# Images 3 and 4 in the 4x4 convolution, later query blocks with the probabilities stationary, and steps placed by an account of emitted work

## The chip, the cores and the metric

The kernel runs on one core of a Trainium2 chip. The metric is the device time of one execution in microseconds (us); the time of a kernel is the median of its runs. The engines are named as the profile names them: PE (TensorE, the matmuls), PEld (its weight loads), DVE (VectorE), ACT (ScalarE), POOL (GpSimd) and SP (SyncE, which here only issues DMAs). Every tensor is float32; PE does one float32 matmul as two passes, and the profile counts passes.

## The reference

Four images of 256 channels and 64x64 pixels go through four layers, each `x = x + layer(groupnorm(x))`:

- layer 0: a 3x3 convolution 256 to 256, group norm, relu (`xs`); then attention over all 4096 pixels with 128 channels, `y = softmax(theta^T phi) g`; a 1x1 convolution back to 256 channels, group norm, times 0.1, plus `xs`.
- layer 1: linear attention with 4 heads of 32 channels; q is normalised over its channels and k over the pixels, `context = k v^T`, `out = context q`, a 1x1 convolution, an RMS norm.
- layer 2: a depthwise 3x3 convolution and a 1x1 convolution whose weights are generated from pooled features of the image.
- layer 3: a 1x1 convolution whose weights are a mixture of 4 experts, with the mixture from a small softmax over the image's mean.

## The kernel before

**Tiles and stages.** Images are numbered b = 0 to 3 in the code. An image is held as 2 halves of 128 channels on the partitions. `convolve_first` does the first image's convolution alone. Then, for b = 0, 1, 2, `attend(b)` (layer 0's attention) runs together with a side chain: `tail(b-1)` (layers 0's end, 1, 2 and 3 of the image before) and the convolution of image b+1. `attend(3)` runs with `tail(2)`; `tail(3)` comes last and alone. Between the stages `project` computes theta, phi and g of the next image.

**Attention.** `attend` has 8 query blocks (q) of 512 pixels and in each 16 steps (m). A step computes the logits of the next step (`pf`, 2 matmuls of 512 columns; ACT takes the exponent into `pr`), then 2 matmuls of 512 columns with 128 columns of g as the stationary operand and `pr` moving, summed into `py` (L1129), and DVE adds `pr` (128x1024) to a running sum `tot`. At a block's end `ended_by_dram` turns the sums of all partitions through DRAM into reciprocals, multiplies `py`, and projects it with `ww` (`ps_wy`); the last block of an image uses `ended` (L1081) instead: a matmul with ones (`pss`), and a reciprocal of 128x512 on DVE. `ended_by_dram` is a generator: one of its steps is taken in each attention step.

**Convolution.** A fast convolution over tiles: `down` combines rows (DVE), `across` combines columns (DVE) into `v`, PE multiplies `v` with transformed filters `u` (`ps_conv`), `joined` and `joining` combine the products back (DVE). The second image's (`convolve_second`) has tiles of 4x4 outputs: 6 rows a x 3 pairs of columns, 8 matmuls of 256 columns for a pair (L601). The third and fourth (`convolve`) have 4x2 outputs: 6 x 4 products of 4 matmuls of 512 columns (L529). In `convolve_second` the output lies in `xp` by phases, and its relu pieces (L698) are 4 ACT instructions of 256 columns; for the other images a piece is one instruction of 1024 (L703). Two of the 8 pieces are issued at the end of the convolution, one after each of the first six steps of `project`.

**The order of the work.** It is written out by hand: each engine executes its instructions in the order in which the Python code issues them. `run(chain, attention)` takes one attention step for each step of the side chain. The side chain is a generator; it yields how many attention steps are to pass, and `Chain.steps` (L82) adds these up, times a rate, and passes whole steps:

```python
credit += n * self.rate
while credit >= 1:
    credit -= 1
    yield
    self.tick()
```

The rates are 1.33 for b = 0, 0.83 for b = 1 and 2, and 1.2 for b = 3. `yield None` passes exactly one step. `w.later(n, f)` issues f after n further steps. `linear_attention` goes through 8 chunks of 512 pixels twice: `qk_of`, `turned`, `context` in the first loop (yields of 1.0 a chunk), `outputs`, `added`, `scaled` in the second (0.6 + 0.6 a chunk). `mixed` computes the softmax of the experts (`ps_log`), mixes the weights on DVE (`wm`, two halves; yields of 2.9 in all), and multiplies (`ps_ex`). For b = 2 `mixed` issues only a small bias matmul (`bias`, `ps_b`) and puts the 16 products into `held`; `tail(3)` takes them out by `fill` where it has gaps.

**Buffers.** There are 8 PSUM banks under one name (`bank`), 9 tiles of 128x1024 (`k4`) and 4 of 128x512 (`k2`).

Of the kernel before, what the change touches and what calls it, by code (L numbers as in the profile page):

```python
# [13 lines left out]
P = 128  # L14
NH = 2
# [23 lines left out]
RW = MX * (IX + 1)  # L39

# [5 lines left out]

class Chain:
# [3 lines left out]
    def __init__(self, layers, rate=1.0, held=()):  # L51
        self.layers, self.rate, self.due = layers(self), rate, []
        self.held, self.unsettled = held, []
# [28 lines left out]
    def steps(self):  # L82
        credit = 0.0
        for part in (self.layers, self.pending()):
            for n in part:
                if n is None:
                    credit += self.rate - 1
                    yield
                    self.tick()
                    continue  # L90
                credit += n * self.rate
                while credit >= 1:
                    credit -= 1
                    yield
                    self.tick()


@with_exitstack
def conv_preact_fast(ctx: ExitStack, tc: tile.TileContext, guard, x, wc, wtpg, ww, wqkv, wout, w1cat, wd2,
# [3 lines left out]
    nc = tc.nc  # L103
    B = x.shape[0]
# [26 lines left out]
    def tt(o, a, b, op):  # L131
        nc.vector.tensor_tensor(o, a, b, op)  # L132

    def stt(o, a, s, b, op0, op1):
        nc.vector.scalar_tensor_tensor(o, a, s, b, op0, op1)  # L135
# [8 lines left out]
    tpg = cp.tile([P, 3, N], F32, name="tpg")  # L144
    ra = cp.tile([P, NH, IY, RW], F32, name="ra")
    rt = cp.tile([P, NH, IY, RW], F32, name="rt")
    theta, phi, g = tpg[:, 0, :], tpg[:, 1, :], tpg[:, 2, :]
# [57 lines left out]
    def block_average(name, k):  # L205

        member = sp.tile([P, P // k], F32, name=name + "_m", bufs=1)
        nc.vector.tensor_reduce(member, ident.rearrange("p (g k) -> p g k", k=k), AX.X, ALU.add)
        t = cp.tile([P, P], F32, name=name)
        nc.vector.tensor_scalar(t.rearrange("p (g k) -> p g k", k=k),  # L210
# [18 lines left out]
    def scale_weights(w):  # L229


        nc.vector.tensor_scalar(bo_s, bo_s, 1.0 / HEADS, None, ALU.mult)

        nc.vector.tensor_scalar(gains, vec_s[:, V_GN:V_GN + 2, :], float(NH * P) ** 0.5, None, ALU.mult)
        for h in range(NH):
            nc.vector.tensor_scalar(wqkv_s[:, h, :], wqkv_s[:, h, :], gains[:, 0, h:h + 1], None, ALU.mult)
# [3 lines left out]
        for h in range(NH):  # L240
            sq = k2("wsq")
            nc.scalar.activation(sq[:, 0:2 * HID], wqkv_s[:, h, 0:2 * HID], AF.Square)
            yield 1
            nc.tensor.matmul(ps[:, 0:2 * HID], ones, sq[:, 0:2 * HID], start=(h == 0), stop=(h == NH - 1))
        wmax = sp.tile([P, 1], F32, name="wmax", bufs=1)
        nc.vector.tensor_reduce(wmax, ps[:, 0:2 * HID], AX.X, ALU.max)
        for side in range(2):
            nc.vector.tensor_scalar(guard[:, side, B * NQ:B * NQ + 1], wmax, GUARD_MAX[side] / NORM2_MAX, None, ALU.mult)

# [4 lines left out]
    tpgf = tpg.rearrange("p k n -> p (k n)")  # L254
# [7 lines left out]
    def filter_down(rows):  # L262

        for h in range(NH):
            w = [taps[:, h, i, :] for i in range(3)]
            if rows == (0,):
                nc.scalar.mul(u1[:, 0, h], w[0], 1 / 4)
            elif rows == (5,):
                nc.scalar.copy(u1[:, 5, h], w[2])
            elif rows == (1, 2):  # L270
                ends, mid = k4("ends")[:, 0:3 * NH * P], k4("mid")[:, 0:3 * NH * P]
                nc.scalar.mul(mid, w[1], 1 / 6)
# [3 lines left out]
            else:  # L276
                far, mid = k4("far")[:, 0:3 * NH * P], k4("mid2")[:, 0:3 * NH * P]
                nc.scalar.mul(far, w[2], 1 / 6)
                nc.scalar.mul(mid, w[1], 1 / 12)
# [8 lines left out]
    def filter_across(a):  # L288
# [9 lines left out]
        nc.scalar.mul(mid, ends[:, :, 1], 0.5)  # L298
# [36 lines left out]
    def stats_tile():  # L335
        return sp.tile([P, NH, 8, 6], F32, name="st")

    def aggregated(st):
        mv = sp.tile([P, NH, 2], F32, name="mv")
        for h in range(NH):  # L340
            nc.vector.bn_aggr(mv[:, h, :], st[:, h, :, :].rearrange("p c s -> p (c s)"))
        return mv

    def warm(n):

        if n:
            ps = bank("ps_warm")
            for i in range(2 * n):
                nc.tensor.matmul(ps[:, 0:P], ones, ident, start=(i == 0), stop=(i == 2 * n - 1))

    def group_finish(st, avg, eps, shift=None, between=(), idle=(0, 0)):
# [12 lines left out]
        nc.tensor.matmul(pm[:, 0:NH], avg, mv[:, :, 0], start=True, stop=True)  # L364
# [5 lines left out]
        nc.vector.tensor_copy(gm, pm[:, 0:NH])  # L370
# [9 lines left out]
        nc.tensor.matmul(pv[:, 0:NH], avg, ev, start=True, stop=True)  # L380
        rstd = sp.tile([P, NH], F32, name="rstd")
        nc.vector.tensor_scalar(rstd, pv[:, 0:NH], eps, None, ALU.add)  # L382
# [12 lines left out]
    def affine(gm, rstd, gw, gb, before, factor):  # L395
# [7 lines left out]
        if factor != 1.0:  # L403
            nc.vector.tensor_scalar(sc, sc, factor, None, ALU.mult)
            nc.vector.tensor_scalar(sh, sh, factor, None, ALU.mult)
# [86 lines left out]
    def load_filter(a, k, last):  # L492

        u = filter_tile("u")
        (nc.scalar if last == 3 else nc.sync).dma_start(out=u, in_=rows_d[a, :, :, 0 if k == 0 else 2] if k in (0, last) else filters[a, :, k - 1])
        return u
# [13 lines left out]
    def joiner(st, factor=None):  # L510
# [4 lines left out]
        def stats(k):  # L515
            for oh in range(NH):
                for s in range(2):
                    nc.vector.bn_stats(st[:, oh, 2 * k + s, :], image[:, oh, bass.ts(s, IY // 2), k, :])
# [5 lines left out]
        def products(a, k, v, u):  # L524

            ps = [bank("ps_conv") for _ in range(NH)]
            for oh in range(NH):
                for h in range(NH):
                    nc.tensor.matmul(ps[oh], u(oh, h), v[:, bass.ts(h, 512)], start=(h == 0), stop=(h == NH - 1))  # L529
                if k == 1:  # L530
                    one[oh] = k2("one").rearrange("p (y x) -> p y x", x=IX1)
                    p = ps[oh].rearrange("p (y x) -> p y x", x=IX1)
                    if factor is None:
                        nc.scalar.copy(one[oh], p)
                    else:
                        nc.scalar.mul(one[oh], p, factor)
# [21 lines left out]
        def row_products(a, rows):  # L558

            banks = []  # L560
            for oh in range(NH):
                if a != 5:
                    take(a, oh)
                for s in range(2):
                    ps = bank("ps_row").rearrange("p (y x) -> p y x", x=HW)
                    for n in range(NH * 3):
                        h, j = divmod(n, 3)
                        nc.tensor.matmul(ps, u1[:, a, h, j * NH * P + oh * P:j * NH * P + (oh + 1) * P],
# [3 lines left out]
                    else:  # L572
                        nc.scalar.copy(dst[oh][:, bass.ts(s, RB), :], ps)
# [11 lines left out]
    def planar_joiner(st):  # L585

        parts = {}

        def stats(k):
            for oh in range(NH):  # L590
                for s in range(2):
                    nc.vector.bn_stats(st[:, oh, 2 * k + s, :], outs[:, oh, k, bass.ts(s, 2), :])

        def products(pair, v, u):

            banks = []
            for i in range(2):
                ps = bank("ps_conv")
                for oh in range(NH):
                    for h in range(NH):  # L600
                        nc.tensor.matmul(ps[:, bass.ts(oh, IY * IX)], u[i][:, h, bass.ts(oh, P)],  # L601
# [1894 lines left out]
```

## Time and profile before

| what | us |
|---|---|
| median of 3 runs (lowest, highest) | 3007.39 (3007.21, 3008.11) |
| the profiled execution | 3005.05 |
| its span, first to last instruction | 3003.3 |
| PE busy / DVE busy / ACT busy in the span | 2953.0 / 2058.4 / 1192.8 |
| attention of image 0 with its side chain | 181.1 to 696.6: 515.5 |
| attention of image 1 with its side chain | 743.6 to 1422.5: 678.9 |
| attention of image 2 with its side chain | 1466.7 to 2145.6: 678.9 |
| attention of image 3 with `tail(2)` | 2189.8 to 2754.0: 564.2 |
| `tail(3)` alone, to the end | 2754.0 to 3003.3: 249.3 |

A line of the profile gives the code line, the engine, the operation, output <- inputs by name and shapes, the number of instructions, the time an engine was busy with them and the mean duration in ns, then the time that the engine sat idle just before them and what it waited for. Matmuls are pipelined: a matmul's duration is longer than the distance to the next, so costs are taken from the distance of starts. In a timeline a row begins with its start and its duration in us and merges equal instructions that follow each other.

### The profile page before, as it was taken

The page shows a single profiled execution, that of the slowest core. Times are in us where ns is not written, and L with a number is a line of the kernel's source. Part 1 is how long each engine was busy: PE and PEld are TensorE (multiplying, and loading weights), DVE is VectorE, ACT ScalarE, POOL GpSimd, SP SyncE. Part 2 cuts the span into 40 slices and gives each one's busy share as a digit, 9 for nine tenths or more (in the row PEclk, how much of TensorE's full clock was granted, in tenths as well). Part 3 has the DMA queues.
Part 4 walks back from the last instruction along what each step waited for, and adds up shares of the span by engine and source line. Part 5 has one row for each costly group of instructions (what it writes and reads, how often), then busy time and mean ns, then how long its engine had stood idle before and what let it go on. Part 6 is the DMA issues. An engine that isn't in the chain of part 4 may idle for free.

```text
span 3003.3 us, 25088 instructions
## 1 busy us (share of the span) xinstructions
PE 2953.0 (98%) x8750; PEld 1511.7 (50%) x8750; DVE 2058.4 (69%) x2835; ACT 1192.8 (40%) x2318; POOL 132.3 (4%) x182
## 2 busy tenths in 40 slices
PE   7999999999999999999999999999999999999998
PEld 3454555555565444444566444444546644444744
DVE  8747667773646994778455797578655468886585
ACT  2234333335456333322455533412335454333732
POOL 0000000001001000000001000000000100000100
PEclk9999999999999999999999999999999999999999
DMA  5245534224402225431610334243431222244021
GB/s 225 76 98 114 60 60 77 39 35 100 90 4 36 32 25 140 86 72 35 161 8 11 53 20 88 78 88 67 89 101 14 25 42 46 28 95 91 22 70 68
DMA packets 536133, 200.58 MB, mean 67 GB/s; under 512 B 471040, under 2 KB 481024, under 8 KB 532480
## 3 DMA queue, kind: packets, MB, share of 16 engines
q1 hardware_dynamic: 127808, 163.25, 17.6%
q10 hardware_dynamic: 403584, 18.88, 12.0%
q0 software_dynamic: 4608, 16.78, 3.7%
q8 instruction: 71, 1.16, 0.2%
q14 instruction: 62, 0.51, 0.1%
HBM read 130.13 MB, written 85.52 MB: 72 GB/s over the span
## 4 chain that ended last, share of the span: by engine, by line
PE 81%; DVE 12%; issue 5%; ACT 1%; POOL 0%; DMA 0%; DVEq 0%; POOLq 0%; ACTq 0%
PE pf L1021 25%; PE py L1129 24%; PE ps_conv L529 5%; PE ps_tp L957 4%; PE ps_qk L1303 3%; PE ps_ex L1804 3%; PE ps_pw L1577 3%; DVE tot L132 2%; DVE dw L135 2%; PE ps_conv L601 2%; PE ps_ctx L1330 2%; PE ps_g L962 2%; PE ps_o L1399 2%; PE ps_wy L1073 2%; PE ps_dw L1624 1%
## 5 line engine op out<-in xcount | busy, mean ns | idle before, releaser
L1022 ACT ACTIVATE pr<-pf 128x512 f32<-128x512 f32 x1024 | 603.1, 596 | 1092.0 <-PE pf L1021 1034.3
L1021 PE MATMUL pf<-tpg 128*128 128x512 f32 x2048 | 966.3, 594 | 0.0
L1129 PE MATMUL py<-pr,tpg 128*128 128x512 f32 x2048 | 961.7, 592 | 0.0
L132 DVE TENSOR_TENSOR tot<-tot,pr 128x1024 f32<-128x1024 f32 x448 | 546.5, 1220 | 181.8 <-ACT pr L1022 181.0
L1129 PEld LDWEIGHTS py<-pr,tpg 128*128 128x128 f32 x2048 | 389.2, 190 | 489.7 <-issue 481.6
L1021 PEld LDWEIGHTS pf<-tpg 128*128 128x128 f32 x2048 | 383.0, 190 | 428.4 <-issue 407.3
L135 DVE SCALAR_TENSOR_TENSOR dw<-xp,dk,dw 128x1008 f32<-128x1008 f32 x208 | 263.1, 1268 | 6.7 <-ACT dw L1569 3.6
L529 PE MATMUL ps_conv<-v,u 128*128 128x512 f32 x384 | 170.9, 593 | 3.2 <-DVE v L132 3.2
L132 DVE TENSOR_TENSOR tpg<-ps_g,bg_s 128x512 f32<-128x512 f32 x32 | 22.1, 692 | 146.9 <-PE ps_g L962 146.9
L529 PEld LDWEIGHTS ps_conv<-v,u 128*128 128x128 f32 x384 | 72.8, 190 | 95.8 <-issue 89.1
L957 PE MATMUL ps_tp<-big,wtpg_s 128*128 128x512 f32 x256 | 116.3, 594 | 2.7 <-ACT big L698 2.0
L225 POOL TENSOR_TENSOR rstd<-rstd,half 128x2 f32<-128x2 f32 x24 | 17.5, 729 | 2194.4 <-DVE rstd L382 2070.5
L1303 PE MATMUL ps_qk<-wqkv_s,xg 128*128 128x256 f32 x496 | 113.1, 379 | 0.0
L1303 PEld LDWEIGHTS ps_qk<-wqkv_s,xg 128*128 128x128 f32 x496 | 94.0, 190 | 21.3 <-issue 8.6
L1577 PE MATMUL ps_pw<-dw,pk 128*128 128x512 f32 x216 | 98.0, 593 | 0.9 <-DVE dw L135 0.9
L958 ACT ACTIVATE tpg<-ps_tp,btp_s 128x512 f32<-128x512 f32 x64 | 44.0, 687 | 95.3 <-PE ps_tp L957 95.3
L957 PEld LDWEIGHTS ps_tp<-big,wtpg_s 128*128 128x128 f32 x256 | 46.6, 190 | 54.5 <-issue 45.2
L1313 ACT ACTIVATE qk<-ps_qk,rinv 128x256 f32<-128x256 f32 x100 | 46.9, 474 | 65.2 <-PE ps_qk L1303 62.9
L962 PEld LDWEIGHTS ps_g<-wtpg_s,big 128*128 128x128 f32 x512 | 62.2, 192 | 15.3 <-issue 15.3
L132 DVE TENSOR_TENSOR v<-ra 128x1024 f32<-128x1024 f32 x58 | 69.2, 1221 | 0.3
L1812 ACT ACTIVATE res<-ps_ex,b 128x512 f32<-128x512 f32 x56 | 38.2, 687 | 76.0 <-PE ps_ex L1804 72.4
L1577 PEld LDWEIGHTS ps_pw<-dw,pk 128*128 128x128 f32 x216 | 40.9, 190 | 53.2 <-issue 49.7
(391 smaller groups left out, 3099.0 us busy)
## 6 DMA issues: line engine op xcount, KB each, us to landing
xp<-in_x_dram SPq DMA_DIRECT2D x16, 1024.0 KB, 8.1
xs_d<-big POOLq DMA_DIRECT2D x32, 512.0 KB, 6.4
wy_d<-wt SPq DMA_DIRECT2D x32, 512.0 KB, 2.8
wy<-wy_d SPq DMA_DIRECT2D x32, 512.0 KB, 4.0
out_dram<-res SPq DMA_DIRECT2D x64, 256.0 KB, 2.0
xs_d<-in_x_dram SPq DMA_DIRECT2D x24, 512.0 KB, 6.0
xs<-xs_d SPq DMA_DIRECT2D x24, 512.0 KB, 4.7
wp<-in_wp_dram SPq DMA_DIRECT2D x16, 512.0 KB, 5.3
```

The lines of the kernel that those rows point to most:

```text
L132: nc.vector.tensor_tensor(o, a, b, op)
L135: nc.vector.scalar_tensor_tensor(o, a, s, b, op0, op1)
L529: nc.tensor.matmul(ps[oh], u(oh, h), v[:, bass.ts(h, 512)], start=(h == 0), stop=(h == NH - 1))
L601: nc.tensor.matmul(ps[:, bass.ts(oh, IY * IX)], u[i][:, h, bass.ts(oh, P)], v[:, i, bass.ts(h, IY * IX)], start=(h == 0), stop=(h == NH - 1))
L957: nc.tensor.matmul(ps, wtpg_s[:, h, k, :], big[:, h, cols], start=(h == 0), stop=(h == NH - 1))
L962: nc.tensor.matmul(ps[:, j, :], big[:, h, bass.ts(4 * c + j, P)], wtpg_s[:, h, 2, :], start=(h == 0), stop=(h == NH - 1))
L1021: nc.tensor.matmul(pf, phi[:, bass.ts(2 * m + s, P)], theta[:, bass.ts(q, 512)], start=True, stop=True)
L1022: nc.scalar.activation(pr[:, bass.ts(s, 512)], pf, AF.Exp)
L1129: nc.tensor.matmul(py, g[:, bass.ts(2 * m + s, P)], probs[i][:, bass.ts(s, 512)], start=(m == 0 and s == 0), stop=(m == NM - 1 and s == 1))
L1303: nc.tensor.matmul(ps[:, 0:2 * HID], xg[:, h, bass.ts(j, P)], wqkv_s[:, h, 0:2 * HID], start=(h == 0), stop=(h == NH - 1))
L1577: nc.tensor.matmul(ps, pk[:, h * NH * P + oh * P:h * NH * P + (oh + 1) * P], dw[h][:, bass.ts(s, 512)], start=(h == 0), stop=(h == NH - 1))
L1804: nc.tensor.matmul(ps, wm[h][:, bass.ts(oh, P)], big[:, h, bass.ts(c, 512)], start=(h == 0), stop=(h == NH - 1))
```

## The change

1. Images 2 and 3 (the third and fourth) go through the 4x4 convolution too: `convolve(w, b, pace)` is the former `convolve_second`, and all three later images have the relu in 4 instructions a piece. Its filters are loaded from SP's queue; the copies of x into `xs_d` move into the first loop of `linear_attention` for images 2 and 3. One more step is passed between two pairs whose products aren't issued (`begun`).
2. In `attend` a block is done "across" if it is the last of its image, or from block 3 on in images 1 and 2 (12 of the 32 blocks): a 128x128 part of the probabilities is the stationary operand, and 129 columns of g move, of which the last is ones. `tot` falls away. `ended` takes the sums from the 129th column, scales, and turns the result with 4 transposes.
3. Statistics move from DVE to ACT: the sums come from `accum_out`, the squares from `Square` on ACT, in `nonlocal_out`, in `pointwise_added` and for three quarters of the convolution's output.
4. Side steps in attention are placed by an account instead of the yielded numbers. Every instruction issued through `on_pe`, `on_dve`, `on_act` adds an estimate of its time. A float yielded by the side chain no longer passes steps; an integer or None passes that many; beyond that, attention steps pass only while DVE or ACT is more than 2 us behind PE in the account. `behind` never falls below -4.

The core of the diff:

```diff
+TURNED = 3
+class Load:
+    SPARE, AHEAD = 2.0, 4.0
+    def add(self, kind, us):
+        if kind == PE:
+            self.products += us
+            for k in (DVE, ACT):
+                self.behind[k] = max(self.behind[k] - us, -self.AHEAD)
+        else:
+            self.behind[kind] += us / self.share[kind]
+    def full(self):
+        return max(self.behind[DVE], self.behind[ACT]) > self.SPARE
+class Metered:
+    def us(self, name, args, kw):
+        if self.kind == PE:
+            n = max(columns(args[2] if name == "matmul" else args[0]), P)
+            return n / (600.0 if name == "matmul" else 1200.0) / (HT if args[0].shape[0] == HP and n > P else 1)
+        n = columns(args[1] if name in ("tensor_reduce", "bn_stats", "bn_aggr") else args[0])
+        if self.kind == DVE:
+            return 0.12 + n * (0.0065 if name == "reciprocal" else 0.0011) + (0.08 if "accum_out" in kw else 0)
+        return 0.12 + n * 0.00102 + (0.19 if "accum_out" in kw else 0)
...
     def steps(self):
+        if self.load is not None:
+            self.load.share, self.load.behind = self.share, [0.0] * 3
         for part in (self.layers, self.pending()):
             for n in part:
...
+                for _ in range(1 if n is None else n if isinstance(n, int) else 0):
                     yield
                     self.tick()
+                while self.load.full():
+                    done = self.load.products
                     yield
                     self.tick()
+                    if self.load.products == done:
+                        break
...
         def piece(c, h):
-            if b == 1:
+            if b > 0:
...
+            if begun:
+                yield 1
+            w.later(1, lambda a=a, pair=pair, v=v, u=u, after=lambda us=us, i=i: load_filter_of(us, i + 1, 1): multiply(a, pair, v, u, after))
+            begun.append(i)
+            yield slow
...
-        def ended(q, py, tot, xc):
+        def ended(q, py, xc):
+            total, r = (sp.tile([P, 4], F32, name=name) for name in ("total", "r_q"))
+            for i in range(2):
+                on_dve.tensor_copy(total[:, bass.ts(i, 2)], py[i][:, :, P])
+            on_dve.reciprocal(r, total)
+            yn = k2("yn")
+            tt(yn[:, 0:2 * P].rearrange("p (t o) -> p t o", o=P), py[0][:, :, 0:P],
+               r[:, 0:2].unsqueeze(2).to_broadcast([P, 2, P]), ALU.mult)
+            for t in range(2, 4):
+                on_act.activation(yn[:, bass.ts(t, P)], py[1][:, t - 2, 0:P], AF.Copy, scale=r[:, t:t + 1])
...
             yield
+            pt, yt = bank("ps_yt"), k2("yt")
+            for t in range(4):
+                on_pe.transpose(pt[:, bass.ts(t, P)], yn[:, bass.ts(t, P)], ident)
...
+        def across(q):
+            return q == NQ - 1 or 0 < b < B - 1 and q >= TURNED
...
+                if across(q):
+                    for t in range(4):
+                        on_pe.matmul(py[t // 2][:, t % 2, :], probs[i][:, s * 512 + t * P:s * 512 + (t + 1) * P], g[:, 2 * m + s, :],
+                                  start=(begin and t % 2 == 0), stop=(end and t % 2 == 1))
+                else:
+                    on_pe.matmul(py, g[:, 2 * m + s, 0:P], probs[i][:, bass.ts(s, 512)], start=begin, stop=end)
...
+    FIRST, MIDDLE, LAST = (1.0, 0.75, 0.9), (1.0, 0.86, 0.91), (1.0, 0.75, 0.85)
-            run(Chain(both(*parts), 1.33 if b == 0 else 0.83).steps(), attention)
+            run(Chain(both(*parts), load, FIRST if b == 0 else MIDDLE).steps(), attention)
-        run(Chain(tail(B - 2, big, qT, held=held), 1.2).steps(), attention)
+        run(Chain(tail(B - 2, big, qT, held=held), load, LAST).steps(), attention)
```

`ended_by_dram` also passes one more step between its multiply on DVE (`yq`) and the projection. The account isn't used in `convolve_first` and in `tail(3)`.

## The prediction

> **What bounds the kernel.** I read the page's busy times and its chain first:
>
> ```profile
> PE 2953.0 (98%) x8750; PEld 1511.7 (50%) x8750; DVE 2058.4 (69%) x2835; ACT 1192.8 (40%) x2318; POOL 132.3 (4%) x182
> ...
> PE 81%; DVE 12%; issue 5%; ACT 1%; POOL 0%; DMA 0%; DVEq 0%; POOLq 0%; ACTq 0%
> ```
>
> Busy PE need not be PE at its peak, so I took from the timeline of PE how far apart matmuls start (start, duration, line, count):
>
> ```profile
> 1124.62 3.60 PE L1577 MATMUL ps_pw<-dw,pk 128*128 128x512 f32 x8
> 1128.05 1.88 PE L1021 MATMUL pf<-tpg 128*128 128x512 f32 x4
> ...
> 1444.13 1.95 PE L962 MATMUL ps_g<-wtpg_s,big 128*128 128x128 f32 x16
> 1445.92 3.60 PE L957 MATMUL ps_tp<-big,wtpg_s 128*128 128x512 f32 x8
> ...
> 2340.59 1.91 PE L1330 MATMUL ps_ctx<-xt,qk 128*128 128x257 f32 x8
> 2342.34 1.89 PE L1303 MATMUL ps_qk<-wqkv_s,xg 128*128 128x256 f32 x8
> 2344.06 1.88 PE L1021 MATMUL pf<-tpg 128*128 128x512 f32 x4
> ```
>
> A pass of 512 columns costs 3.43/8 = 0.429 us, of 256 columns 1.72/8 = 0.215 (0.216 over all), of 257 columns 0.219, of 128 columns with a new weight load each 1.79/16 = 0.112; a transpose pass 0.109. Summing these prices over the recorded passes gives 2920 of 3003 us, and in the four attention stages the starts follow each other at these distances but for some 5 us a stage. The waits of PE say the same (us in total, times, longest):
>
> ```profile
> PE ps_conv L529 <- DVE v L132: 3.2, 2, 1.6
> PE pv L380 <- DVE ev L132: 2.5, 6, 0.8
> PE ps_wy L1073 <- DVE yq L132: 2.2, 2, 1.1
> PE ps_tp L957 <- ACT big L698: 2.0, 3, 0.7
> ```
>
> So the time is PE's work plus PE's few waits. Less DVE work gains nothing by itself; what counts is how many passes go or come, and whether PE still finds its operands ready.
>
> [...] the trace has 190 ns a load, yet 112 ns from load to load. [...]
>
> **Part 1, the convolution.** By-form groups of PE:
>
> ```profile
> L529 PE MATMUL ps_conv<-v,u 128*128 128x512 f32 x384 | 170.9, 593 | 3.2 <-DVE v L132 3.2
> L601 PE MATMUL ps_conv<-v,u 128*128 128x256 f32 x288 | 65.1, 379 | 0.0
> ```
>
> An image goes from 192 passes x 0.429 = 82.4 to 288 x 0.216 = 62.2 us; two images: **-40.4**. DVE's combining grows from 68 instructions of 1024 columns at 1.22 and 48 of 512 at 0.69 (116 us) to 50 and 120 (144 us) an image; attention's own PE work hides it, and uncovered it would be 28 us an image. The relu in four pieces: in the second image's `project` PE waits at `ps_tp` for ACT's `big` L698 in three places, 2.5 us beyond the distance of starts; the images with one instruction a piece have none. Two more images: **+5.0**. Filter loads take 3.1 us to landing and products lie at least 7 apart (a step of 3.43 and their own 3.46): nothing. The copies into `xs_d` (6 us each on SP's queue) move into a stretch in which SP has nothing that PE waits for: nothing; late, they would hold the first reload of a block's sums.
>
> **Part 2, across.** One step of a half: 2 passes x 0.429 = 0.858 become 4 x 2 passes of 129 columns. No row shows 129. From `ps_g` (0.112) and the step from 256 to 257 columns I take 0.113: 0.904, +0.045. [...] 12 blocks x 32 = 384: **+17.3** (+8 to +33). Transposes 12 x 4 x 0.109 = +5.2, the four `pss` pairs gone -3.4: **+1.8**. DVE loses 12 x 15 adds of 1.22 = 220 us, worth nothing on PE. At the very end `fill(2)` (3.43 us) now stands between the transposes and `ps_wy`; before, it stood behind `ps_wy` and covered the reciprocal of 3.36. Last statistics about **+2** (0 to 3).
>
> **Part 3, statistics.** Twice in a tail, 16 `Square`s with their accumulator reads (0.72 + 0.19, as L1595 in the last image) replace 16 `bn_stats` of 0.69. That is 29 us more of ACT a tail beside 675 us of PE, of which ACT is busy for 266 now; it would count only before the sums are read, where a forced step of 3.43 stands. Nothing.
>
> **Part 4, the account.** I added up the side chains with the diff's own formulas. For b = 0 DVE has 352 us, /0.75 = 469, under 492 of PE; for b = 1 and 2 it is 429/0.86 = 499 under 632 (the rest are forced steps); for b = 3 354/0.75 = 472 under 524. All end before attention does (after 118 to 122 of 128 steps), so nothing runs over; an overrun would cost its DVE time. But where PE's side work pays for ACT's and DVE's in the account, no step passes at all, and `behind` forgets that DVE can't start until PE's newest product is there. Three places:
>
> (a) `mixed`. The two forced steps before leave `behind` at -4. After `ps_log` DVE gets 4.36 us of account, /0.86 = 5.1: `behind` reaches 1.1, under 2, no step; with 0.75 it reaches 1.8, no step either. Before, 2.9 x 0.83 = 2.4 steps stood there. What the wait is without steps, the last image shows, where held products fill it:
>
> ```profile
> 2961.53 0.38 PE L1765 MATMUL ps_log<-rw_s,hb 64*128 64x4 f32 x2
> ...
> 2965.21 0.29 DVE L132 TENSOR_TENSOR wm<-wm,ident 128x128 f32<-128x128 f32 x1
> 2965.42 0.35 DVE L1785 TENSOR_SCALAR wm<-ex,scales 128x256 f32<-128x256 f32 x1
> ...
> 2967.36 0.29 DVE L132 TENSOR_TENSOR wm<-wm,ident 128x128 f32<-128x128 f32 x1
> ```
>
> First half ready after 4.0 us, second after 6.1. For the tails of images 0 and 1 PE waits 4.0 - 0.2 = 3.8 (the first half's products then cover the second); for image 2 `bias` needs both: 5.9. PE's queue behind it, attention included, waits. **+13.5**.
>
> (b) Second loop of `linear_attention`. Before, one step (3.43) stood in each chunk:
>
> ```profile
> 896.14 1.04 PE L1429 MATMUL ps_zt<-ident,z 128*128 128x128 f32 x8
> ...
> 897.02 1.89 PE L1399 MATMUL ps_o<-w,xp 128*128 128x256 f32 x8
> 898.75 1.88 PE L1021 MATMUL pf<-tpg 128*128 128x512 f32 x4
> 900.46 1.88 PE L1129 MATMUL py<-pr,tpg 128*128 128x512 f32 x4
> 902.18 1.04 PE L1429 MATMUL ps_zt<-ident,z 128*128 128x128 f32 x8
> ```
>
> PE's own work is 2.6 a chunk. ACT's loop is longer: four squares 2.04, DVE and POOL 1.25, `scaled` 0.8, together 4.1. A chunk gives the account 3.5 us of DVE, /0.86 = 4.1, against 2.6 of PE, so the credit of 4 carries the first three chunks (two for b = 2) and one late one without a step. The first `z` is ready 5.2 after its `ps_o` starts, when PE has had 3.5 of work: 1.7; then 4.1 - 2.6 = 1.5 each; half of that late. 1.7 + 1.5 + 1.5 + 0.8 = 5.5 for b = 1 and again for b = 2; for the chain of b = 3, 3.2: **+14.2** (0 to 25).
>
> (c) First loop: 6.5 us of PE a chunk (16 passes of 0.216, 12 transposes of 0.109, 8 passes of 0.219) against a loop of 6.1 from transposes through squares, POOL, DVE's two `xt` and its normalising, 7.0 where POOL's `pow` takes 1.9; PE's 6.5 exceed ACT's 5.1/0.91 in the account, so no step passes at all. 1 us a tail: **+3** (0 to 10).
>
> Gone, by the distance of starts: 1.27 us at `ps_wy` (extra step) and 1.78 at the first `ps_conv`, in two stages each, **-6**.
>
> **Sum.** -40.4 + 5.0 + 17.3 + 1.8 + 2 = -14.3 of work and fixed waits; 13.5 + 14.2 + 3 - 6 = +24.7 of waits. Span 3003.3 + 10.4 = 3013.7. The median shown stands 4.1 above the profiled span (3007.39 - 3003.3): **3018 us**, own range 3008 to 3030.
>
> **Rivals.** My new waits sum to 30.7 us. Up to 14.3 the kernel ends faster by 6 or more, above 26.3 slower by 6; my forecast stands only 4.4 beyond. *PE stays fed*: the places of part 4 cost nothing, because PE comes to them with its queue full and DVE and ACT ahead, and only the old waits go. For it: alone, in the last image, the first loop ran its later chunks without a wait. Against it: PE is in order and can't overtake a product that waits. 3007.4 - 14.3 - 6.0 = 2987, and with some 4 us of small waits, as a stage has now, **2991**: faster. *Weight loads show*: with sixteen loads in a row for whole blocks, 129 columns cost 0.118: 384 x 8 x 0.005 = +15, 3033; at 0.125, 3055. `ps_g` speaks against it, but only in bursts of 16. *Waits for banks*: two `py` leave six PSUM banks for all else across, and four at a block's change; a wait of 0.2 us in every second of the 192 steps is +19, 3037. Against it: `py` and `ps_ctx` leave six already, without waits. *The account does nothing*: can't be; 2.4 steps in `mixed` become none by arithmetic.
>
> **Chances.** A measurement can tell about 0.2% (6 us) from no change. Forecast 0.52 (of it 0.07 within 6 us of before, 0.02 faster), PE stays fed 0.27 (0.21 faster, 0.05 same, 0.01 slower), weight loads 0.12, buffers 0.09 (0.04 of these two the same, 0.01 faster). Faster 0.24, same 0.16, slower 0.60. Range: 2988 takes in the fed case, 3038 the lesser half of the other two: 2988 to 3038.
>
> **What would show it.** Right: 576 `ps_conv` passes of 256 columns 0.216 apart and none at 512 in images 2 and 3; `py` across 0.113 apart; waits of `ps_zt` for `z`, and of `ps_ex` and `ps_b` for `wm`, of 4 to 6 us each in the list of PE's waits; `ps_tp` waits for `big` 9 times; no `pf` among the chunks of the first loop. Wrong: attention steps inside `mixed`, an attention stage of image 1 much below 680 us (I have 678.9 - 20.2 + 7.2 + 1.3 + 7.2 = 674.4), or PE's busy starts 0.12 apart in across blocks.

## The result and the profile after

The kernel after takes 3049.61 us (median of 4 runs, 3047.57 to 3053.32), the kernel before beside it 3007.75 (3007.21 to 3008.27): a ratio of 1.0142, 95% interval 1.013 to 1.0155. It is slower by 42 us. The profiled execution took 3053.32 us, the longest of the four; its span is 3051.5: 48.2 more than before.

The page of the kernel after, busy times and two groups of PE (out<-in, shapes, count, then busy time and mean ns, then PE's idle time ahead of them). Every metered operation now has the line of the helper that records it, L99, so the groups go by names:

```profile
PE 2950.8 (97%) x11286; PEld 1762.6 (58%) x11286; DVE 1833.7 (60%) x2808; ACT 1335.4 (44%) x2674; POOL 121.1 (4%) x185
...
L99 PE MATMUL py<-tpg,pr 128*128 128x129 f32 x3072 | 377.6, 277 | 10.4 <-ACT pr L99 10.4
...
L99 PE MATMUL ps_conv<-v,u 128*128 128x256 f32 x864 | 197.8, 382 | 5.8 <-DMA u<-rows_d 3.2
```

DVE lost 225 us of work, as the change has it, and PE's busy time hardly moved. But priced by pass, as in the prediction (0.4295 for 512 columns, 0.216 for 256 or 257, 0.112 for 128 or 129, 0.109 for a transpose), PE's work fell from 2919.9 to 2895.4 us, by 24.5. What lies beyond these prices between the starts rose from 60.2 to 132.3, by 72.1. All of the loss, and more, is waiting or slow passes. The list of PE's waits (us in total, times, longest) says where:

```profile
PE pm L99 <- DVE mv L99: 23.3, 6, 16.9
PE ps_zt L99 <- DVE z L99: 15.5, 9, 2.8
PE py L99 <- ACT pr L99: 11.9, 6, 5.2
PE ps_ex L99 <- DVE wm L99: 7.3, 2, 3.6
PE ps_b L99 <- DVE wmh L99: 5.1, 2, 3.6
PE ps_tp L99 <- ACT big L99: 4.7, 7, 0.7
PE ps_zt L99 <- ACT junk L99: 4.5, 2, 2.3
PE ps_xt L99 <- DVE xg L99: 3.4, 3, 1.2
PE ps_conv L99 <- DMA u<-rows_d: 3.2, 2, 2.3
```

The first row stood there before too, with 22.2 us. The waits for `z`, `wm`, `wmh` and `xg` are among those forecast. Those of `py` for `pr` and of `ps_conv` for a filter were not.

The wait in `mixed`, tail of image 0, in the timeline of PE, and the same stretch by windows (length, busy time and count by engine, granted clock of PE ahead of the DMA share):

```profile
1138.11 0.38 PE L99 MATMUL ps_log<-rw_s,hb 64*128 64x4 f32 x2
1142.13 5.30 PE L99 MATMUL ps_ex<-big,wm 128*128 128x512 f32 x8 [3.64 <-DVE wm L99]
```

```profile
core 0: us, PE busy (x) PEld busy (x) DVE busy (x) ACT busy (x) POOL busy (x), PEclk, DMA share, GB/s
1138.60:1142.00 3.40, 0.00 (x0) 0.00 (x0) 2.77 (x11) 0.35 (x2) 0.00 (x0) 1.00 0.00 0
1142.00:1145.40 3.40, 3.27 (x4) 1.52 (x5) 2.09 (x6) 0.00 (x0) 0.00 (x0) 0.50 0.00 0
```

`ps_ex` starts 4.02 after `ps_log`, of which 0.16 is the pass itself: 3.86 of wait, three times in the run. And then something that the prediction has nowhere: in the 3.4 us after the wait PE's granted clock is 0.50 and only 4 passes of 512 columns fit in, where 8 would at 0.4295 each. Before, the recorded clock has no such window between the first microseconds and the last; now it has 13, in 11 stretches, in mid-run, and by the passes in them they cost 18.4 us.

The second new wait, in the timeline of ACT and PE, where image 2's convolution begins:

```profile
1188.01 8.69 ACT L99 ACTIVATE big<-xp,nb,rstd 128x1024 f32<-128x1024 f32 x4 [2.56 <-DVE nb L99]
```

```profile
1188.38 1.95 PE L99 MATMUL py<-tpg,pr 128*128 128x129 f32 x16
1190.16 1.88 PE L99 MATMUL pf<-tpg 128*128 128x512 f32 x4
1197.23 3.81 PE L99 MATMUL py<-tpg,pr 128*128 128x129 f32 x16 [5.19 <-ACT pr L99]
1200.83 3.17 PE L99 MATMUL pf<-tpg 128*128 128x512 f32 x4
```

Four pieces of `normalise_planar` stand in ACT's queue ahead of attention's exponent, 8.69 us: it starts at 1196.59, behind the last piece, though the `pf` it reads ran from 1186.58 for 1.96 us. `py` waits 5.35. Again the passes after it go at half clock: 16 passes of 129 columns take 3.60 from start to start (1200.83 - 1197.23), and 1.78 before the wait (1190.16 - 1188.38), 0.111 a pass.

### The profile page after: what moved, and what is told of

Same layout as the page of the kernel before. It is cut to its first block, busy times and chain, and to the rows that moved or that the text cites. A ratio compares the mean times of both kernels' runs of the same rounds, so it can differ in the third digit from the quotient of the medians.

```text
span 3051.5 us, 30579 instructions
## 1 busy us (share of the span) xinstructions
PE 2950.8 (97%) x11286; PEld 1762.6 (58%) x11286; DVE 1833.7 (60%) x2808; ACT 1335.4 (44%) x2674; POOL 121.1 (4%) x185
## 4 chain that ended last, share of the span: by engine, by line
PE 85%; issue 6%; DVE 4%; ACT 3%; DMA 2%; POOL 1%; SPq 0%; POOLq 0%; DVEq 0%; ACTq 0%
PE py L99 28%; PE pf L99 27%; PE ps_conv L99 6%; PE ps_ex L99 4%; PE ps_tp L99 4%; PE ps_pw L99 3%; PE ps_qk L99 3%; PE ps_wy L99 2%; PE ps_ctx L99 2%; PE ps_g L99 2%; PE ps_dw L99 1%; ACT big L99 1%; ACT junk L99 1%; PE ps_o L99 1%; DVE st L99 1%
## 5 line engine op out<-in xcount | busy, mean ns | idle before, releaser
L99 ACT ACTIVATE pr<-pf 128x512 f32<-128x512 f32 x1024 | 601.0, 596 | 976.9 <-PE pf L99 951.4
L99 PE MATMUL pf<-tpg 128*128 128x512 f32 x2048 | 973.8, 599 | 0.0
L99 PE MATMUL py<-pr,tpg 128*128 128x512 f32 x1280 | 602.3, 593 | 1.5 <-ACT pr L99 1.5
L99 PEld LDWEIGHTS pf<-tpg 128*128 128x128 f32 x2048 | 378.8, 192 | 380.4 <-issue 367.1
L99 DVE TENSOR_TENSOR tot<-tot,pr 128x1024 f32<-128x1024 f32 x280 | 342.1, 1222 | 170.8 <-ACT pr L99 170.3
L99 PEld LDWEIGHTS py<-tpg,pr 128*128 128x128 f32 x3072 | 376.4, 194 | 101.7 <-issue 84.4
L99 PEld LDWEIGHTS py<-pr,tpg 128*128 128x128 f32 x1280 | 243.9, 191 | 309.5 <-issue 298.1
L99 PE MATMUL py<-tpg,pr 128*128 128x129 f32 x3072 | 377.6, 277 | 10.4 <-ACT pr L99 10.4
L99 DVE SCALAR_TENSOR_TENSOR dw<-xp,dk,dw 128x1008 f32<-128x1008 f32 x208 | 263.1, 1269 | 7.0 <-ACT dw L99 3.6
L99 PE MATMUL ps_conv<-v,u 128*128 128x256 f32 x864 | 197.8, 382 | 5.8 <-DMA u<-rows_d 3.2
L99 PEld LDWEIGHTS ps_conv<-v,u 128*128 128x128 f32 x864 | 162.3, 191 | 36.8 <-issue 11.6
L99 PE MATMUL ps_tp<-big,wtpg_s 128*128 128x512 f32 x256 | 117.1, 596 | 4.7 <-ACT big L99 4.7
L99 DVE TENSOR_TENSOR tpg<-ps_g,bg_s 128x512 f32<-128x512 f32 x32 | 22.1, 692 | 155.2 <-PE ps_g L99 155.2
L99 PE MATMUL ps_qk<-wqkv_s,xg 128*128 128x256 f32 x496 | 112.1, 379 | 0.0
L99 PEld LDWEIGHTS ps_qk<-wqkv_s,xg 128*128 128x128 f32 x496 | 94.0, 190 | 13.8 <-issue 1.4
L99 PE MATMUL ps_pw<-dw,pk 128*128 128x512 f32 x224 | 101.0, 593 | 0.0
L99 DVE SCALAR_TENSOR_TENSOR sums<-ps_conv,sums 128x512 f32<-128x512 f32 x72 | 49.8, 691 | 77.1 <-PE ps_conv L99 65.5
L99 DVE BATCH_NORM_STATS2 wy_st<-wt 128x6 f32<-128x512 f32 x64 | 43.8, 692 | 74.4 <-ACT wt L99 73.9
L99 PEld LDWEIGHTS ps_tp<-big,wtpg_s 128*128 128x128 f32 x256 | 45.9, 191 | 54.6 <-issue 42.3
L99 ACT ACTIVATE tpg<-ps_tp,btp_s 128x512 f32<-128x512 f32 x64 | 44.0, 687 | 70.5 <-PE ps_tp L99 70.5
L99 ACT ACTIVATE res<-ps_ex,b 128x512 f32<-128x512 f32 x56 | 38.1, 688 | 79.1 <-PE ps_ex L99 77.2
```

The lines of the kernel that those rows point to most:

```text
L99: return f(*args, **kw)
```

## The experiments

Differences below are to the changed kernel's median, 3049.7 (3049.61, and 3049.77 when it ran again), each with the ratio to the kernel before on the same chip.

**Theory.** The account lets no step pass where PE's side work pays for DVE's and ACT's, PE runs into the wait of `mixed`, of the second loop of `linear_attention` and of `normalise_planar`, and each of these waits costs a second time through half clock. **Rivals.** Steps are a fixed stock (128 an image), so that a wait mended at one place comes up at another; the waits come from the new work itself (the planar convolution, the across blocks), whatever places it; half clock is a side effect without a price.

**Steps in `mixed`.**

```diff
                 if j % 2 == 1:
-                    yield 0.6
+                    yield 1 if w.load is not None and h == 0 else 0.6
```

> The changed kernel, but two attention steps are forced inside `mixed` between the first half's scaled experts and its first product (tails of images 0, 1, 2). Theory, zero steps: the three waits behind ps_log (3.86 us each, and 1.66 more for the second half in the tail of image 2) go, and with them the three stretches of half TensorE clock after them (1.6, 1.4 and 2.5 us lost): 3 x 3.86 + 1.66 + 5.4 = 18.6 us less, 3031. If only the waits count and the half clock is no cost of theirs: 3036. Rival, the waits only move, because the steps spent here are missing later: 3045 to 3052.

Measured: 3029.64 us, ratio 1.0074 (1.0057 to 1.0091), 20 us less where 18.6 were expected. In PE's timeline the same place now holds attention:

```profile
1137.60 0.38 PE L99 MATMUL ps_log<-rw_s,hb 64*128 64x4 f32 x2
1137.92 1.98 PE L99 MATMUL pf<-tpg 128*128 128x512 f32 x4
...
1145.03 1.45 PE L99 MATMUL ps_ex<-big,wm 128*128 128x512 f32 x3
```

Two steps are forced, and the chain ends one step later, after 123 of 128: the account passes one step fewer further on. So the steps were there to be had, and the rival of a fixed stock falls at this place. The two timelines also show that what stands behind a waiting product waits with it: issued ahead of `ps_ex`, `pf` starts 0.32 us after `ps_log`; issued behind it, no pass at all runs for 3.86 us.

**Steps in the second loop of `linear_attention`.**

```diff
             zb = outputs(c)
             root(zb[0])
-            yield 0.6
+            yield 1 if c in range(NC) else 0.6
```

> The changed kernel, but one attention step is forced in each of the eight chunks of the second loop of linear_attention (tails of images 0, 1, 2). Theory, zero steps: the waits of ps_zt for z (7.5, 8.6 and 4.6 us) go, and the four stretches of half clock after them (1.3, 1.7, 1.6, 1.5 us lost): 20.7 + 6.1 = 27 us less, 3023. Waits alone: 3029. Rival, the steps are missing later or the loop is held by something else than its lack of steps: above 3040.

Measured: 3025.69 us, ratio 1.0064 (1.0047 to 1.0081), 24 us less where 27 were expected. No wait of `ps_zt` for `z` over 0.5 us is left in the tails of images 0 to 2. The waits of `mixed` stand where they were (7.3 us of `ps_ex` for `wm`), and `py`'s longest is 5.7 for 5.2.

**Steps between the pieces of `normalise_planar`.**

```diff
                     on_act.activation(to, src, AF.Identity, bias=nb[:, h:h + 1], scale=rstd[:, h:h + 1])
-            yield 0.6
+            yield 1 if q in (0, 1, 2) else 0.6
```

> The changed kernel, but an attention step is forced after each of the first three of the four pieces of normalise_planar. Theory: the 5.35 us for which py waits for pr in images 1 and 2 come from ACT, which has four copies of 2.17 us queued ahead of attention's Exp; with a step between the pieces both waits go, and the half clock after them (2.95 and 1.40 us lost): 10.7 + 4.4 = 15 us less, 3035. Rival, py waits for another reason (banks, DVE): 3047 to 3052.

Measured: 3034.12 us, ratio 1.0093 (1.0077 to 1.011), 15.6 us less where 15 were expected. `py` waits for `pr` no longer at this place. The account prices such a piece on ACT at 0.12 + 1024 x 0.00102 = 1.16 us; it took 8.69/4 = 2.17.

**Copies moved.** The copies of image 1 into `xs_d` go out of the convolution's loop:

```diff
-            if b == 1 and i % 3 == 2 and i < 12:
-                copy_x(b, i // 3)
...
             if a + 2 < TY:
                 loaded.append(load(a + 2))
+            if a < 4:
+                copy_x(1, a)
```

> The changed kernel, but the eight copies of image 1 into xs_d leave the convolution's loop and are issued in filters_across, four times two, earlier in the same attention stage. Theory: the four waits of ps_conv in the stage of image 0 (0.75, 1.04, 2.48, 2.16 us, each some 5 us after a copy) come from a filter load queued behind 2 x 512 KB on SP; they go, with 1.5 us of half clock after the last: 8 us less, 3042. Rival, the products simply lie too close to their loads or to DVE's operands: the waits stay, 3047 to 3052.

Measured: 3043.15 us, ratio 1.0118 (1.0102 to 1.0135), 6.5 us less; the stage of image 0 goes from 526.1 to 517.8 us, 8.3 less, and all four waits are gone. In the changed kernel, SP's and PE's timelines at one of the four, the filter load stands behind two copies and lands when PE has waited 2.3 us:

```profile
438.68 1.19 SPq L807 DMA_DIRECT2D xs_d<-in_x_dram  x2
...
440.60 0.57 SPq L609 DMA_DIRECT2D u<-rows_d  x1
```

```profile
447.48 1.97 PE L99 MATMUL ps_conv<-v,u 128*128 128x256 f32 x8 [2.32 <-DMA u<-rows_d]
```

Issued at 440.60, used at 447.48: 6.9 us, where the 72 filter loads of images 2 and 3 have a median of 2.6 to landing.

**PE kept busy in the waits.** No step moves; only idle time of PE is filled with products that nobody reads:

```diff
+    def kept_busy(n):
+        if n:
+            ps = bank("ps_warm")
+            for i in range(2 * n):
+                nc.tensor.matmul(ps[:, 0:P], ones, ident, start=(i == 0), stop=(i == 2 * n - 1))
...
         w.settle()
+        kept_busy(0 if alone else 8)
         first = [bank("ps_ex") for _ in range(4)]
...
             if last is not None:
+                kept_busy(4 if c in (1, 2, 6) and (c < 6 or b < 2) else 0)
                 added(c - 1, last)
```

and 8 before `bias` of image 2, and 16 before the `py` that follows `normalise_planar`.

> The changed kernel with its waits left in place: every step, wait and operand stands where it did, and only products of 128 columns into an unused bank (16, 8 or 32 of 0.112 us) are put into the waits of mixed, of the second loop of linear_attention and of the copies of normalise_planar, so that TensorE isn't idle there. They shorten nothing and are shorter than the waits. Theory, half clock: a window of 3.41 us that is idle for more than about 0.63 is followed by a window at half clock, and these are worth 15.9 us in sum: 3034. Rival, the half clock isn't set off by these waits, or costs nothing: 3049 to 3053, or later where the products overrun a wait.

Measured: 3041.66 us, ratio 1.0114 (1.0097 to 1.0131), 8 us less, half of what was expected. A float32 product is two passes (16 products stand in this run's timeline of `mixed` as `ps_warm` x32, from 1135.39 to 1139.10), so what was put in was twice as long as meant; at `py` it overran the wait by 1.8 us, twice. With less put in (6 and 11 for 8 and 16):

> As the run that keeps TensorE busy in the waits, with less put in: a float32 product is two passes, so that 16 and 32 products were 3.6 and 7.2 us and the latter overran its wait of 5.35 by 1.8, twice. Now 12, 8 and 22 products: 2.7, 1.8 and 4.9 us, all shorter than the waits they stand in, but for the wait of 1.67. Theory, half clock: 15.9 us are to be had; about 1.2 go to chunks whose wait was shorter than what is put in and 1.4 to a half window that may stay at the bias of image 2: 13 us less than the changed kernel, 3036. Rival, the 8 us of the first try came from something else and half clock is worth less: 3041 or more.

Measured: 3038.68 us, ratio 1.0105 (1.0087 to 1.0123), 11.1 us less than the changed kernel, which was run again beside it. PE's timeline in `mixed`:

```profile
1134.07 0.38 PE L99 MATMUL ps_log<-rw_s,hb 64*128 64x4 f32 x2
1134.38 2.95 PE L427 MATMUL ps_warm<-ident,ones 128*128 128x128 f32 x24
1138.09 3.70 PE L99 MATMUL ps_ex<-big,wm 128*128 128x512 f32 x8 [0.77 <-DVE wm L99]
```

`ps_ex` starts 4.02 after `ps_log`, exactly as before, but now its 8 passes run at 0.43 each. PE does 32 us of passes more than the changed kernel and ends 11 us earlier. No wait was mended here; the products only fill idle time. So half clock has a price of its own, in this kernel these 11.1 us, and here it was idle PE that set it off: of 13 windows in mid-run 3 are left, and the mean granted clock is 0.998 where it was 0.992. The expected 13 us were not quite reached.

**The changed kernel again.**

> The changed kernel as it is, on the same chip and beside the run before it. Both: 3047 to 3054 again, 3049.6 in the middle. If the windows of half clock are what spreads it, the spread is some 5 us again, and the windows of this trace lie on another phase than those of the first.

Measured: 3049.77 us (3046.09 to 3051.85), ratio 1.014 (1.0122 to 1.0159). The windows of half clock lie on a grid of 3.413 us whose phase against the kernel's start is 1.46 us here (mean granted clock 0.991) and 1.93 in the first trace (0.992); they cost 17.7 and 18.4 us, partly after other waits. The runs spread by 5.8 us, those of the kernel before by 1.9, those of the kept-busy one by 1.5. That the phase makes the spread is likely from this, not shown.

**All four mends.** The account's share of DVE in the middle chains goes from 0.86 to 0.90, so that the chains end inside attention.

```diff
-    FIRST, MIDDLE, LAST = (1.0, 0.75, 0.9), (1.0, 0.86, 0.91), (1.0, 0.75, 0.85)
+    FIRST, MIDDLE, LAST = (1.0, 0.75, 0.9), (1.0, 0.9, 0.91), (1.0, 0.75, 0.85)
```

> All four mends at once: forced steps in mixed, in the second loop of linear_attention and in normalise_planar, and the copies moved; the account's share of DVE in the middle chains goes from 0.86 to 0.90, so that the chains end inside attention (after 125 of 128 steps). Theory: what each mend brought alone adds up, 20 + 24 + 15.5 + 8 = 67 us less, 2982, faster than the kernel before by 0.8 per cent. Rival, steps are a fixed stock and what is spent at one place is missing at another, so that new waits come up: 3000 and above.

Measured: 2981.41 us (2980.71 to 2981.73), ratio 0.9914 (0.9898 to 0.9931), 68 us less than the changed kernel and 26 less than the kernel before. The single mends sum to 20.1 + 24.0 + 15.6 + 6.5 = 66.2. Beyond the prices of the passes there are 60.8 us left, as in the kernel before (60.2), and the gain over it is about the 24.5 us of PE's work. The attention stage of image 1, by windows:

```profile
743.90:1407.90 664.00, 661.26 (x2956) 435.09 (x2956) 415.35 (x651) 311.81 (x638) 31.77 (x36) 1.00 0.24 59
```

It was 678.9 us before and 688.0 after the change; here it is 664.0 with PE busy for 661.3.

**The rates of before instead of the account.** Parts 1 to 3 stay; `Chain.steps` is that of before.

```diff
-    FIRST, MIDDLE, LAST = (1.0, 0.75, 0.9), (1.0, 0.86, 0.91), (1.0, 0.75, 0.85)
+    FIRST, MIDDLE, LAST = 1.33, 0.8, 1.2
...
-            parts = [tail(b - 1, big, qT), lambda w: convolve(w, b + 1, 0.53)] if b > 0 else [
+            parts = [tail(b - 1, big, qT), lambda w: convolve(w, b + 1, 0.4)] if b > 0 else [
```

> The changed kernel without its account: the chains are stepped by the rates of before again (1.33, 0.80 where it was 0.83, and 1.2; pace of the middle convolution 0.40 so that it ends after 126 steps). Parts 1 to 3 stay. Theory, the loss is the account's placing: work is 24.5 us less than before, some 4 us of waits in project stay, small waits elsewhere: 2987, the waits behind ps_log and ps_o gone. Rival, the planar convolution and the across blocks bring the waits themselves: 3020 and above.

Measured: 3012.94 us (3008.68 to 3014.88), ratio 1.0019 (1.001 to 1.0028): 37 us less than with the account, but 26 more than expected. The waits behind `ps_log` are gone; others take their place, the largest for ACT. Its timeline at the head of a tail:

```profile
763.84 0.72 ACT L99 ACTIVATE junk<-big,about 128x512 f32<-128x512 f32 x1
...
768.80 1.06 ACT L99 ACTIVATE pr<-pf 128x512 f32<-128x512 f32 x2
```

Six of the new `Square`s stand here ahead of the next exponent, which starts at 768.80, and `py` waits 2.36 for it, in image 1 and again in image 2. The rate counts steps without knowing that this work has moved from DVE to ACT; the account does know. So each way of placing steps has its blind spots. With the account mended in its three places the kernel is 31.5 us faster than with the rates, of which the copies make 6.5. Rates tuned for this kernel were not tried.

**Fewer across blocks, twice.** `TURNED = 7` leaves one across block in an image instead of five for images 1 and 2; once with the rates, and once with all four mends (there with a share of 1.1 for DVE, since with DVE's 146 us more the chains would otherwise outlast attention).

```diff
-TURNED = 3
+TURNED = 7
```

> As the run with the rates of before, but the five blocks a middle image that are turned become one: eight across blocks fewer, with DVE's 15 sums of 1.22 us a block back. Theory, an across block costs PE 1.37 us more ((14.6 + 1.8)/12): 11 us less than with the rates alone, 2976. Rival, DVE's 146 us more make it late for PE's operands: as long as the rates alone or longer.

> The run with all four mends, but with one across block a middle image instead of five; the account's share of DVE in the middle chains is 1.1, because with DVE's 146 us more the chains would otherwise not end inside attention. Theory, across blocks cost PE and their relief of DVE is worth nothing: 8 blocks x 1.6 us (13 us by the passes of the run with rates) less, 2968. Rival, seen with the rates: without them DVE (588 of some 665 us an image) is late for the convolution's operands, and the planar convolution needs the relief: 2990 to 3015.

Measured: 3034.46 us, ratio 1.0092 (1.0075 to 1.0109), 21.5 more than the rates alone; and 3013.22 us, ratio 1.0019 (1.001 to 1.0028), 31.8 more than the four mends. PE's passes do fall, by 13.0 us both times (11 and 13 were expected). But among PE's waits stand, with the rates and with the mends:

```profile
PE ps_conv L99 <- DVE v L99: 19.0, 8, 4.9
```

```profile
PE ps_pw L99 <- DVE dw L99: 14.3, 4, 3.9
PE py L99 <- ACT pr L99: 13.7, 13, 2.2
PE ps_conv L99 <- DMA u<-filters: 6.5, 4, 2.0
```

DVE comes late for `v` and `dw`, and PE's clock is halved again in 7 and 5 windows of mid-run, against 2 and 1 (mean granted clock 0.995 and 0.997, against 0.998 in both). With the mends PE also waits for `pr` and for filters (0.9 and 0.2 us without this edit), and the share was changed too, so that not all of the 31.8 us is shown to be DVE's. Under both ways of placing steps the across blocks bring more than their 13 us of PE. Whether some other pacing could do with fewer across blocks wasn't found out: only these two were tried, and each was made for the other number of blocks.

**Two more waits.** On top of the four mends:

```diff
-        for _ in range(NH):
+        for _ in range(2 * NH if b else NH):
             relus.pop(0)()
             yield None
...
                 copy_x(b + 2, c // 2)
-            yield 0.5
+            yield 1 if c == 0 and w.load is not None else 0.5
```

> The run with all four mends, and besides: four pieces of the relu instead of two are done before project begins (two forced steps more at the end of a convolution), and one step is forced in the first chunk of the first loop of linear_attention. Theory, the relu in four instructions a piece is what ps_tp waits for in project (0.83 twice an image, three images) and the first chunk's transposes wait 1.32 for want of a step (three tails): 5.0 + 4.0 = 9 us less, 2972. Rival, the relu waits only move to other columns, or the two steps are missing elsewhere: 2977 to 2985.

Measured: 2977.99 us (2977.33 to 2978.27), ratio 0.9905 (0.9889 to 0.9922), 3.4 us less than the four mends: the fastest of all. The relu half held: each `project` goes from 45.8 to 43.9 us and no `ps_tp` waits for `big` any more in them, 5.6 in sum. The other half did not: the three waits of `ps_xt`, 1.31 each, stand as they were, so it isn't the lack of this step that makes them. In the trace DVE's half of `xg` stands behind `xt`, which waits 1.12 us for POOL's `rinv`; the step was forced ahead of that, and none was tried behind it. Two waits of 1.2 us at `py`, at the end of the longer convolution, are new.

## Why the prediction was wrong

It said 3018, with a range of 2988 to 3038, slower at 0.60; it is 3049.61. The sign and most of the mechanisms were right, the size was not. Four steps failed: "Three places" without a step, where a fourth cost 11.5 us; "nothing" for the copies, which cost 6.4; the waits of (b), followed along ACT's loop where DVE's `z` comes last, 6.5 short; and each wait priced at its own length, where half clock after it cost 18.4 more. By its own terms, in us of the span:

| term of the sum | predicted | in the trace after |
|---|---|---|
| conv of images 2, 3 | -40.4 | -40.4 |
| relu in 4 pieces, `project` | +5.0 | +2.6 |
| across: passes and transposes | +17.3, +1.8 | +15.9 |
| end of the last block | +2 | +1.8 |
| (a) `mixed` | +13.5 | +13.2 |
| (b) second loop | +14.2 | +20.7 |
| (c) first loop | +3 | +3.1 |
| old waits gone | -6 | -6.1 |
| exponent behind `normalise_planar` on ACT | none | +11.5 |
| filter loads behind the copies on SP | 0 | +6.4 |
| half clock after waits | none | +18.4 |
| sum (span: 48.2) | +10.4 | +47.1 |

**Part 1.** The passes are right: 576 of 256 columns at 0.216 in images 2 and 3, none of 512. The relu's step was mis-sized: `project` waits at two `ps_tp` of 0.83 an image, not at three (2.8 us beyond the prices before, 3 x 1.8 after). "The copies into `xs_d` ... nothing" failed: I looked only for what the copies of images 2 and 3 move into. In the stage of image 0 the copies of image 1 stayed where they were, but products now follow each other 6.9 us apart and a step is forced between them, so that the second filter's load is issued behind the copies; before, the products lay 10 to 15 us apart there. The prediction's own "filter loads take 3.1 us to landing" doesn't hold behind the copies, where the four loads took 5.6 to 7.0 us. The run with the copies moved shows it.

**Part 2.** 0.113 a pass was 0.111 to 0.112; the rival *weight loads show* is refuted. The lower end of the range, +8, stands for 0.110 a pass, and as an estimate the trace before gives that: 429 ns for 512 columns and 216 for 256, at a granted clock of 1.00, leave 213 ns for 256 columns, so 129 columns come to 216 - 127 x 213/256 = 110. The upper end, +33, stands for 0.118, which no trace showed. "DVE loses 220 us, worth nothing on PE" was wrong as a statement on the change: the two runs with fewer across blocks lost 21.5 and 31.8 us where PE's passes alone would have won 13.

**Part 3.** "Nothing" holds in the changed kernel. With the rates of before it would not have: 2.4 us an image at `py`.

**Part 4.** (a) is right to 0.3 us, by the duration read from the last image's timeline. (b) has the right cause, no step, but the wrong path, and is 6.5 short: 7.5, 8.6 and 4.6 us against 5.5, 5.5 and 3.2. The second chunk's wait is 2.92, where I had 1.5 from ACT's loop. Its timeline:

```profile
882.32 0.84 ACT L99 ACTIVATE z<-ps_o,zr 128x256 f32<-128x256 f32 x2 [1.32 <-POOL zr L297]
882.49 0.73 DVE L99 SCALAR_TENSOR_TENSOR big<-ps_zt,gains,big 128x512 f32<-128x512 f32 x1
...
883.26 0.69 DVE L99 BATCH_NORM_STATS2 st<-big 128x6 f32<-128x512 f32 x1
...
883.87 0.67 DVE L99 TENSOR_TENSOR z<-ps_o,zr 128x512 f32<-128x512 f32 x1
...
884.60 1.09 PE L99 MATMUL ps_zt<-ident,z 128*128 128x128 f32 x8 [2.76 <-DVE z L99]
```

ACT's half of `z` is done at 883.16. DVE's half stands behind the chunk before, two sums into `big` and two `st`, and is done at 884.54, 1.38 later: this is what the estimate left out. (c) has its size: one wait of 1.31 a tail behind `rinv` and `xt`, less the 0.79 that stood there before. The `pow` of 1.9 us that it allowed for didn't come: `rinv` took 1.01, 31 times of 32, as it did before. In the trace before, a `pow` of 128x4 took 1.8 to 1.9 us 18 times, each time beside a `tot` addition on DVE.

Missed altogether is a fourth place with no step, `normalise_planar`: I searched the account where PE's side work pays for DVE's and ACT's, and here PE has none. By the diff's formulas a piece counts 1.25/0.86 = 1.45 us of DVE; from the credit of 3.7 that the forced step ahead leaves, the first three pieces pass no step, and the account takes for ACT about half of what a piece costs there. The trace before has four of these pieces already, at 2.29 us each (`big<-xp,nb,rstd`). Whether attention's exponent is queued behind it was the question to ask of each stretch without a step, on ACT as well as on PE.

**Half clock.** No term for it, and the largest of the misses. The prediction took from the trace before the price of a pass alone; there the granted clock is 1.00 until PE's last pass. In the trace after, 13 windows of 3.413 us in mid-run have 0.50, and PE was idle for only part of the window ahead of most of them (from 0.61 of its length on, below). With the four places in the sum, 3013.7 + 6.5 + 11.5 + 6.4 + 18.4 = 3056.5, less 2.4 and 3.2 for the terms that came out smaller: 3050.9, where 3051.5 was measured.

**The rivals.** *PE stays fed* (2991) is wrong for the kernel as it stands, but about right for what the change can give: with steps where they are needed, and the copies moved, it is 2981 to 2978. *Waits for banks* doesn't appear among PE's waits. The forecast for the stage of image 1, 674.4, came out at 688.0: 5.35 for ACT, 7.5 for half clock and 2.0 in the second loop make 14.9 where 13.6 are missing.

## What to carry to other kernels

When instructions are placed by an account of their own durations, look for the stretches in which no step of the other stream passes at all, and ask on every engine, not on the bottleneck alone, what then stands ahead of the other stream's next instruction (here 8.69 us of ACT ahead of an exponent); at the three places mended here forced steps brought the whole wait back while steps were left. A wait of some 2 us or more on TensorE cost, in the changed kernel, about 1.4 us on top for each window of half clock after it (18.4 us for 13), and was uncertain by that much. An engine's relief can be worth more than its price on the bottleneck if another part of the same change leans on it, so parts of a change are not to be priced one by one alone.

## What was not expected of the hardware

- PE's granted clock fell to 0.50 for one window of 3.413 us (twice for 6.83, from 1196.59 and from 2770.14) after a window in which PE was mostly, not wholly, idle. By the distances of starts in the trace of the changed kernel, leaving out the first 25 and the last 12 us, PE was idle for 0.61 to 1.00 of the window ahead of each of the 11 stretches, and in no other window at full clock for more than 0.58. With the traces of the 12 runs above added: all 73 windows idle for 0.65 or more of their length were followed by one; of those between 0.60 and 0.65, 9 of 17; below that only windows that were at half clock themselves. This takes passes of 1 to 16 columns at 0.02 us each, an estimate (two of `pm` or `pv`, 128x2, start 0.03 apart); at 0.06 the border blurs to between 0.55 and 0.65 over all runs. So in these runs a wait of some 2.2 us (0.65 x 3.413) that fell into one window was followed by half clock.
- Such a window cost mostly 1.3 to 1.7 us in the changed kernel. The grid lay elsewhere against the kernel's start in the two traces of the changed kernel (1.93 and 1.46 us), and a wait of 2 to 3 us was followed by such a window in one run and not in another: of the changed kernel's four waits of 2.92 and 2.48 us, two were in the first trace (2.92 to 884.60 and to 2356.00; not those to 447.48 and to 1618.35), and the other two in the second.
- The `Identity` of 128x1024 with a stride in its input took ACT 2.17 us from start to start (2.26 each by its record); one of the same size without a stride (`xp<-xp,nb,rstd`) took 1.23 by its record in the same trace.
